# A graph layer on one core: loads three ahead and evictions two behind in a background job, and zero rows written one at a time beside another job

## The chip, the cores and the metric

The kernel runs on one core of a Trainium2 chip. The metric is the device time of one execution in microseconds; the median of the runs is given. Times that are read off a profile come from one profiled execution. The engines are PE (matrix multiply; PEld is its weight load), DVE (vector), ACT (scalar functions), POOL (here the issuer of the indirect DMAs) and SP (the issuer of the plain DMAs).

## The reference

For 6250 nodes with 256 features, and 206,250 edges sorted by destination, the layer computes:

```
xn = layernorm(x)
q, k, v = xn Wq + bq, xn Wk + bk, xn Wv + bv            (8 heads of 32)
per edge (src -> dst): sim = q[dst] . k[src] * scale;  p = softmax over the edges of dst
agg[dst] = sum of p * v[src];  gnn = agg Wo + bo
mix: linear attention over all nodes, 8 heads of 64: k and v instance-normalised,
     dots = k^T v, out = q dots / N, then its projection
x  = x + gnn + mix
h  = layernorm(x); each node goes to the one of 8 experts with the largest logit
     (capacity 977); y = (relu(h W1 + b1) W2 + b2) * probability
out = x + y
```

## The kernel before

**Blocks and groups.** The nodes stand in 49 blocks of 128, in three groups of 20, 17 and 12 blocks. First a node stage (to about 137 us) computes keys and values of all blocks into the DRAM table `kv_tab`, the queries of the first group alone, and sorts the first group's nodes by degree. Then the attention over edges runs through the blocks of group 0, 1 and 2. In a group's blocks the nodes stand in order of degree, so that a block needs a planned number of edge slots `S`.

**Units and chunks.** A block with more than 44 slots is cut into units; a unit is cut into chunks of at most 5 slots (`W`), seven or eight chunks a unit. Per slot POOL issues one indirect gather of 128 rows (2 KB: key and value) into one of 11 (`RING`) buffers `kvg` (line 627). DVE multiplies the chunk's keys with the query (L1373) and reduces over the heads (L1374); this is the score. When all chunks of a unit are scored comes its softmax (L1379 to L1404, with ACT's exponential L1391). In the next unit's chunks DVE weighs the values chunk by chunk (`weigh`, L1325) and PE adds them up with an identity matrix (L1329), which frees the ring's buffer. `complete` then makes `ag` (L1347) and `send` scatters it to `agg_tab` (L843, on POOL's queue). POOL's program holds the gathers up to two chunks (`LEAD`) beyond the one that is scored ahead of that scatter.

**Background jobs.** All other work is written as generators in a list `jobs`, which are taken in order, one after the other. Before and after the weighing of each chunk the main loop calls `background(work / 2)`. Each `yield n` of a job costs n credits; `background` runs jobs while it has credit, and sets the credit to zero when the list is empty. `pace` (L1295) gives the credit per slot: for group 0 it is 1.1 x 363.8 (`work_beside(0)`) over 693 slots, so 0.58 a slot and 2.9 a chunk of five. Nothing but this order and the semaphores decides when an instruction runs[...].

For group 0 the jobs are:

1. `other_queries` (L649): the queries of blocks 20 to 48. Per block: SP loads the transposed block `xTm` (L661, 128 KB, two buffers), PE multiplies it in two halves (L672) into a PSUM bank (five buffers, shared by all jobs), DVE scales and adds the bias into `qn` (L675, two buffers), and SP stores it to `q_tab` (L678). A turn for block b loads b + 1, multiplies b and evicts b - 1.
2. `other_ranks` (L681): orders groups 1 and 2 by degree, mostly DVE work (L282 to L362, `over` L687).
3. `zero_rows` (L692): writes zeros to the DRAM buffers `xbuf` that the experts' tokens are scattered into later. Three rows of 1 KB per partition and write, so 30 writes of 384 KB or less on SP (L701), one credit each, 11.1 MB in all.
4. `linear_attention` (L704): loads its weights `wm`, subtracts column means (L727 to L729) and row means (L233), then for 49 blocks loads `xTm` (L719), projects (L751), squares on ACT, takes variances on DVE (L768 to L777), scales on ACT and multiplies (L788). A step is two yields of 2.4.

When a group's last block is sent, the job `behind(g)` is appended: output projection, routing, scatter to `xbuf` (`to_tiles`), the experts, and `finish`. It runs beside the attention of the next group; that of the last group runs alone after the attention.

Of the kernel before, what the change touches and what calls it, by code (L numbers as in the profile page):

```python
# [9 lines left out]
F32 = mybir.dt.float32  # L10
# [3 lines left out]
ALU = mybir.AluOpType  # L14
# [4 lines left out]
P = 128  # L19
# [9 lines left out]
GROUPS = (20, 17, 12)  # L29
# [39 lines left out]
def gps_layer(  # L69
# [34 lines left out]
    nc = tc.nc  # L104
    N, D = x.shape
    E = n_edges
    NB = -(-N // P)
# [6 lines left out]
    DC = D // P  # L114
# [3 lines left out]
    NX, _, F = w1.shape  # L118
# [14 lines left out]
    def q_rows(b):  # L133

        i = b - FIRST_OF[group_of[b]]
        return q_tabs[group_of[b]][i * P : (i + 1) * P, :]

    def bcast_row(ap, n, parts=P):
        return bass.AP(tensor=ap.tensor, offset=ap.offset, ap=[[0, parts], [1, n]])
# [18 lines left out]
    with tc.manual_schedule():  # L158
# [36 lines left out]
        rstd = keep.tile([P, NB], F32, name="rstd")  # L195
# [8 lines left out]
        def x_transposed(to, b, n=1, queue=nc.sync):  # L204

            queue.dma_start(to, xT_all[:, b * DC * P : (b + n) * DC * P])
# [7 lines left out]
        def bank(shape):  # L214

            t = bps.tile([P, 512], F32, name="bank")
            n = math.prod(shape)
            v = t[:, :n]
            if len(shape) == 2:
                v = v.rearrange("p (a b) -> p a b", a=shape[0])  # L220
            if len(shape) == 3:
                v = v.rearrange("p (a b c) -> p a b c", a=shape[0], b=shape[1])
            return v

        def less_mean(w, n):

            for c0 in range(0, n, 512):
                m = min(512, n - c0)
                pw = bank((m,))
                for c in range(DC):  # L230
                    nc.tensor.matmul(pw, ones_d, w[:, c, c0 : c0 + m], start=(c == 0), stop=(c == DC - 1))
                for c in range(DC):
                    nc.vector.tensor_sub(w[:, c, c0 : c0 + m], w[:, c, c0 : c0 + m], pw)  # L233


        jobs = []
# [408 lines left out]
        bctx = ExitStack()  # L645
        mp1 = bctx.enter_context(tc.tile_pool(name="m1", bufs=1))
        mp2 = bctx.enter_context(tc.tile_pool(name="m2", bufs=2))

        def other_queries():  # L649

            wq = mp1.tile([P, DC, D], F32, name="wqn")
            for c in range(DC):
                nc.sync.dma_start(wq[:, c, :], w_node[c * P : (c + 1) * P, 2 * D : 3 * D])
            bq = mp1.tile([P, D], F32, name="bqn")
            nc.sync.dma_start(bq, bcast_row(b_node[2 * D :], D))
            xT_of, pq_of = {}, {}

            def load(b):
                if b < NB:
                    xT_of[b] = mp2.tile([P, DC, P], F32, name="xTm")  # L660
                    x_transposed(xT_of[b].rearrange("p c q -> p (c q)"), b)  # L661

            load(GROUPS[0])
            yield 2.0
            less_mean(wq, D)
            yield 2.0
            for b in range(GROUPS[0], NB + 1):
                load(b + 1)
                if b < NB:
                    pq_of[b] = bank((D,))  # L670
                    for c in range(DC):
                        nc.tensor.matmul(pq_of[b], xT_of[b][:, c, :], wq[:, c, :], start=(c == 0), stop=(c == DC - 1))  # L672
                if b > GROUPS[0]:
                    q = mp2.tile([P, D], F32, name="qn")
                    nc.vector.scalar_tensor_tensor(  # L675
                        q, pq_of.pop(b - 1), rstd[:, b - 1 : b], bq, op0=ALU.mult, op1=ALU.add
                    )
                    nc.sync.dma_start(q_rows(b - 1), q)  # L678
                yield 1.0

        def other_ranks():  # L681
            t = rank_consts(mp1)
            for g in range(1, NG):
                yield from rank_group(g, t, mp1, mp2)
            bs = list(range(NB))
            for b in bs:
                nc.vector.tensor_scalar(over[:, b : b + 1], deg_r[:, b : b + 1], float(SLOTS[b]), None, op0=ALU.is_gt)  # L687
                if b % 8 == 7:
                    yield 1.5
            nc.vector.tensor_reduce(bad[:, 1:2], over, AX.X, ALU.max)  # L690

        def zero_rows():  # L692

            zero = mp1.tile([P, D], F32, name="zero")
            nc.vector.memset(zero, 0.0)
            for g in range(NG):
                n_r = TILES[g] * SIZE[g] // P
                view = xbufs[g][0 : n_r * P, :].rearrange("(p r) d -> p r d", p=P)
                for r in range(0, n_r, 3):
                    n = min(3, n_r - r)  # L700
                    nc.sync.dma_start(view[:, r : r + n, :], zero[:, None, :].to_broadcast([P, n, D]))  # L701
                    yield 1.0

        def linear_attention():  # L704
# [9 lines left out]
            xT_of = {}  # L714

            def load(b):
                if b < NB:
                    xT_of[b] = mp2.tile([P, DC, P], F32, name="xTm")
                    x_transposed(xT_of[b].rearrange("p c q -> p (c q)"), b)  # L719
# [26 lines left out]
            def project(b):  # L746
                pms[b] = []
                for s in range(2):
                    pm = bank((MI,))
                    for c in range(DC):  # L750
                        nc.tensor.matmul(  # L751
                            pm, xT_of[b][:, c, :], wmf[:, c, s * MI : (s + 1) * MI],
                            start=(c == 0), stop=(c == DC - 1),
                        )
                    pms[b].append(pm)

            def squares(b):
                sqs[b] = mp2.tile([P, G, MD], F32, name="sq")
                for s in range(2):
                    nc.scalar.activation(  # L760
                        sqs[b][:, s * MH : (s + 1) * MH, :].rearrange("p g d -> p (g d)"), pms[b][s], AF.Square
                    )
                cvs[b] = mp2.tile([P, MI], F32, name="cv")
                nc.scalar.copy(cvs[b], pms[b][1])

            def variances(b):
                rv = mp2.tile([P, G], F32, name="rv")
                nc.vector.tensor_reduce(rv, sqs[b], AX.X, ALU.add)  # L768
                nc.vector.tensor_scalar(rv, rv, rs2[:, 1, b : b + 1], EPS, op0=ALU.mult, op1=ALU.add)
                rks[b] = mp2.tile([P, MH], F32, name="rk")  # L770
                nc.vector.tensor_mul(rks[b], rv[:, :MH], rv[:, MH:])
                nc.scalar.activation(rks[b], rks[b], AF.Sqrt)

            def scaled(b):
                rk = rks[b]
                nc.vector.reciprocal(rk, rk)
                nc.vector.tensor_scalar(rk, rk, rs2[:, 0, b : b + 1], None, op0=ALU.mult)  # L777
                cks[b] = mp2.tile([P, MH, MD], F32, name="ck")
                for h in range(MH):
                    nc.scalar.activation(  # L780
                        cks[b][:, h, :], pms[b][0][:, h * MD : (h + 1) * MD], AF.Copy, scale=rk[:, h : h + 1]
                    )

            def products(b):
                ckf = cks[b].rearrange("p h d -> p (h d)")
                for hp in range(HP):
                    h = slice(hp * P, (hp + 1) * P)
                    nc.tensor.matmul(  # L788
                        dots[:, hp, :], cvs[b][:, h], ckf[:, h],
                        start=(b == 0 and hp == 0), stop=(b == NB - 1 and hp == HP - 1),  # L790
                        skip_group_check=True,
                    )

            for i in range(NB + 2):
                if 2 <= i:
                    products(i - 2)
                load(i + 1)
                if i < NB:
                    project(i)
                if 1 <= i <= NB:  # L800
                    variances(i - 1)
                yield 2.4
                if i < NB:
                    squares(i)
                if 1 <= i <= NB:
                    scaled(i - 1)
                yield 2.4

            wq = mp1.tile([P, HP, D], F32, name="wq")
            nc.sync.dma_start(wq, w_mixq.rearrange("(h p) d -> p h d", p=P))  # L810
            wot = mp1.tile([P, HP, D], F32, name="wot")
# [470 lines left out]


        jobs.append(other_queries())
        jobs.append(other_ranks())
        jobs.append(zero_rows())
        jobs.append(linear_attention())

        def work_beside(g):
# [672 lines left out]
```

## Time and profile before

| what | value |
|---|---|
| median of 3 runs | 3531.13 us (3529.72 to 3541.31) |
| profiled execution, its own time | 3071.36 us |
| span, first to last instruction | 3069.6 us |
| PE busy | 2217.7 us (72%) |
| DVE busy | 2026.7 us (66%) |
| POOL busy | 1923.8 us (63%), 2114 instructions |
| ACT busy | 638.1 us (21%) |
| DMA | 728.05 MB, mean 237 GB/s |
| mean granted PE clock | 0.855 |

The profiled execution is 460 us shorter than the median of the runs. The busy times are averages over stages. In the trace the first key and value gather starts at 138.4 us, the queries job runs to 241 us, the ranks to 351 us, the zero rows are issued from 352 to 397 us, and the linear attention follows. A line of the timeline gives start, length, engine, line, operation and count, and in brackets how long the engine was idle before, and what released it.

### The profile page before, as it was taken

How to read it: one execution, taken by the hardware profiler on the slowest of the kernel's cores; microseconds unless marked ns; L12 is line 12 of the kernel's file. 1: busy time of each engine (PE TensorE's matmuls, PEld its weight loads, DVE VectorE, ACT ScalarE, POOL GpSimd, SP SyncE). 2: the span in 40 equal slices, each digit the busy share in tenths (PEclk: the TensorE clock that was granted, in tenths of full speed). 3: DMA queues.
4: the chain of work that ended last, by engine and by line, in shares of the span. 5: the costliest groups of instructions: out<-in, count | busy, mean ns of one | idle time of the engine just before them, and what ended most of it. 6: DMA issues, size and time to landing. Idle time of an engine off the chain costs nothing. (4 is left out here: it accounts for less than half of the span.)

```text
span 3069.6 us, 29584 instructions
## 1 busy us (share of the span) xinstructions
PE 2217.7 (72%) x9090; PEld 1731.0 (56%) x9090; DVE 2026.7 (66%) x2728; ACT 638.1 (21%) x1800; POOL 1923.8 (63%) x2114
## 2 busy tenths in 40 slices
PE   8756548788788655764989988445629999856494
PEld 4335335555555444643777877334528888735494
DVE  5658868898888767884767766566845666664000
ACT  4300003343434101210111111101202122112242
POOL 4366767777777777567777777776466767650101
PEclk9867779999898778876999999678859999978797
DMA  7675876777777668767888887777668988753783
GB/s 256 212 248 171 268 260 201 213 211 213 208 206 221 199 197 262 250 195 234 307 285 307 294 301 248 223 204 248 198 188 279 321 300 311 241 179 111 279 327 111
DMA packets 294378, 728.05 MB, mean 237 GB/s; under 512 B 47142, under 2 KB 156292, under 8 KB 280900
## 3 DMA queue, kind: packets, MB, share of 16 engines
q0 software_dynamic: 149744, 477.83, 50.7%
q1 hardware_dynamic: 144468, 248.24, 23.2%
q8 instruction: 75, 1.23, 0.2%
q14 instruction: 91, 0.75, 0.1%
HBM read 652.25 MB, written 73.64 MB: 236 GB/s over the span
## 5 line engine op out<-in xcount | busy, mean ns | idle before, releaser
L627 POOL DMA_INDIRECT kvg<-kv_tab,idx x1715 | 1628.3, 949 | 650.7 <-issue 463.2
L1329 PE MATMUL pa<-kvg,ident 128*128 128x256 f32 x3430 | 1008.4, 451 | 583.3 <-DVE kvg L1325 420.6
L1329 PEld LDWEIGHTS pa<-kvg,ident 128*128 128x128 f32 x3430 | 756.9, 227 | 817.1 <-DVE kvg L1325 501.4
L1373 DVE TENSOR_TENSOR kvg<-kvg,qc 128x1280 f32<-128x1280 f32 (+1 forms) x366 | 512.4, 1400 | 389.3 <-DMA kvg<-kv_tab,idx 326.7
L1374 DVE TENSOR_REDUCE sim<-kvg 128x40 f32<-128x1280 f32 (+1 forms) x366 | 513.2, 1402 | 12.6
L1325 DVE TENSOR_TENSOR kvg<-kvg,pr 128x1280 f32<-128x1280 f32 (+1 forms) x366 | 509.3, 1393 | 0.0
L1204 PE MATMUL bank<-wt,hTe 128*128 128x256 f32 x1056 | 247.7, 382 | 0.0
L1187 PE MATMUL bank<-xTe,wt 128*128 128x256 f32 x1056 | 242.6, 381 | 2.3 <-ACT xTe L1177 2.3
L1187 PEld LDWEIGHTS bank<-xTe,wt 128*128 128x128 f32 x1056 | 201.6, 191 | 30.5 <-ACT xTe L1177 3.0
L1204 PEld LDWEIGHTS bank<-wt,hTe 128*128 128x128 f32 x1056 | 201.7, 193 | 27.5
L1268 DVE TENSOR_TENSOR res<-bank,row_b 128x256 f32<-128x256 f32 x49 | 20.6, 421 | 280.8 <-ACT bank L1264 272.6
L751 PE MATMUL bank<-wm,xTm 128*128 128x512 f32 x392 | 178.0, 597 | 0.0
L1247 POOL DMA_INDIRECT row_a<-ybuf,row_from x49 | 46.5, 948 | 197.6 <-DMA ybuf<-res 173.0
L1193 ACT ACTIVATE hTe<-bank,wt 128x256 f32<-128x256 f32 x264 | 110.8, 471 | 266.0 <-PE bank L1187 266.0
L1210 ACT COPY res<-bank 128x256 f32<-128x256 f32 x85 | 31.7, 372 | 424.5 <-PE bank L1208 236.1
L751 PEld LDWEIGHTS bank<-wm,xTm 128*128 128x128 f32 x392 | 72.1, 194 | 71.6 <-issue 71.3
L1301 ACT COPY qc<-qs 128x256 f32<-128x256 f32 x49 | 18.8, 384 | 442.9 <-DVE kvg L1373 412.0
L843 POOL DMA_INDIRECT xbuf<-row_a,row_to x49 | 48.0, 980 | 96.6 <-DVE cmp L1088 67.5
L537 PE MATMUL pkv<-wn,xT 128*128 128x512 f32 (+1 forms) x276 | 106.0, 540 | 3.5 <-DVE kv L552 3.5
L843 POOL DMA_INDIRECT agg_tab<-ag,node_ri x49 | 48.5, 990 | 91.2 <-DVE ag L1347 68.4
L1173 PE MATMUL bank<-ident,in 128*128 128x128 f32 x170 | 28.7, 283 | 100.4 <-DMA in<-xbuf 100.4
L780 ACT ACTIVATE ck<-bank,rk 128x64 f32<-128x64 f32 x392 | 86.2, 341 | 28.9 <-DVE rk L777 28.4
(258 smaller groups left out, 2208.4 us busy)
## 6 DMA issues: line engine op xcount, KB each, us to landing
wt<-in_w_rows_dram SPq DMA_DIRECT2D x33, 1152.0 KB, 8.2
wt<-in_w_rows_dram SPq DMA_DIRECT2D x33, 1028.0 KB, 7.9
kvg<-kv_tab,idx POOLq DMA_INDIRECT x1715, 4.0
kvg<-in_w_rows_dram SPq DMA_DIRECT2D x19, 1152.0 KB, 6.1
kvg<-in_w_rows_dram SPq DMA_DIRECT2D x19, 1028.0 KB, 7.7
kv_tab<-kv SPq DMA_DIRECT2D x49, 256.0 KB, 2.7
in<-xbuf SPq DMA_DIRECT2D x85, 128.0 KB, 8.7
ybuf<-res SPq DMA_DIRECT2D x85, 128.0 KB, 3.4
```

Of the source, the lines that this page charges most:

```text
L537: nc.tensor.matmul(done[i], xTs[b // GX][:, b % GX, c, :], wn[:, c, w], start=(c == 0), stop=(c == DC - 1))
L627: nc.gpsimd.indirect_dma_start(out=kv[:, j - j0, :], out_offset=None, in_=kv_tab[:, :], in_offset=bass.IndirectOffsetOnAxis(ap=idx_of[b][: ...
L751: nc.tensor.matmul(pm, xT_of[b][:, c, :], wmf[:, c, s * MI : (s + 1) * MI], start=(c == 0), stop=(c == DC - 1),)
L780: nc.scalar.activation(cks[b][:, h, :], pms[b][0][:, h * MD : (h + 1) * MD], AF.Copy, scale=rk[:, h : h + 1])
L843: s = nc.gpsimd.indirect_dma_start(**kw)
L1187: nc.tensor.matmul(ph[:, k, :], w[:, c, f * P : (f + 1) * P], T[t]["xT"][:, c, :size], start=(k == 0 and c == 0), stop=(k == 1 and c == DC ...
L1193: nc.scalar.activation(T[t]["hT"][:, f, :size], ph[:, k, :], AF.Relu, bias=w1_t[:, V1 + f : V1 + f + 1])
L1204: nc.tensor.matmul(py, T[t]["hT"][:, f, k * P : (k + 1) * P], w[:, f, :], start=(f == 0), stop=False)
L1325: nc.vector.tensor_tensor(vals, vals, v["pr"][:, j0 - s0 : j1 - s0, :, None].to_broadcast([P, m, GH, GD]), ALU.mult)
L1329: nc.tensor.matmul(v["pa"], ident, kv[:, j, D:], start=(j0 + j == s0), stop=(j0 + j == s1 - 1),)
L1373: nc.vector.tensor_tensor(keys, keys, qc[:, None, :].to_broadcast([P, j1 - j0, D]), ALU.mult)
L1374: nc.vector.tensor_reduce(sim[:, j0 - s0 : j1 - s0, :], keys.rearrange("p j (h d) -> p j h d", d=GD), AX.X, ALU.add)
```

## The change

In `other_queries` the loads get a pool of four buffers of their own (`xTq`) and run three blocks ahead of the matmul instead of one; the eviction and the store are two blocks behind it instead of one, with one more turn of the loop and so one more credit. `zero_rows` is no longer a job of its own: `linear_attention` takes one of its 30 writes at the start of each of its 51 steps, ahead of that step's load of `xTm`, and what is left at the end. The writes themselves are the same, and cost no credits now. `work_beside(0)`, and with it the pace, is unchanged.

```diff
         mp2 = bctx.enter_context(tc.tile_pool(name="m2", bufs=2))
+        mp4 = bctx.enter_context(tc.tile_pool(name="m4", bufs=4))
...
             def load(b):
                 if b < NB:
-                    xT_of[b] = mp2.tile([P, DC, P], F32, name="xTm")
+                    xT_of[b] = mp4.tile([P, DC, P], F32, name="xTq")
                     x_transposed(xT_of[b].rearrange("p c q -> p (c q)"), b)
 
-            load(GROUPS[0])
+            for b in range(GROUPS[0], GROUPS[0] + 3):
+                load(b)
             yield 2.0
             less_mean(wq, D)
             yield 2.0
-            for b in range(GROUPS[0], NB + 1):
-                load(b + 1)
+            for b in range(GROUPS[0], NB + 2):
+                load(b + 3)
                 if b < NB:
                     pq_of[b] = bank((D,))
                     for c in range(DC):
                         nc.tensor.matmul(pq_of[b], xT_of[b][:, c, :], wq[:, c, :], start=(c == 0), stop=(c == DC - 1))
-                if b > GROUPS[0]:
+                if b > GROUPS[0] + 1:
                     q = mp2.tile([P, D], F32, name="qn")
                     nc.vector.scalar_tensor_tensor(
-                        q, pq_of.pop(b - 1), rstd[:, b - 1 : b], bq, op0=ALU.mult, op1=ALU.add
-                    )
-                    nc.sync.dma_start(q_rows(b - 1), q)
+                        q, pq_of.pop(b - 2), rstd[:, b - 2 : b - 1], bq, op0=ALU.mult, op1=ALU.add
+                    )
+                    nc.sync.dma_start(q_rows(b - 2), q)
                 yield 1.0
...
+            zeros = zero_rows()
             for i in range(NB + 2):
+                next(zeros, None)
                 if 2 <= i:
                     products(i - 2)
                 load(i + 1)
...
+            for _ in zeros:
+                pass
             wq = mp1.tile([P, HP, D], F32, name="wq")
...
         jobs.append(other_queries())
         jobs.append(other_ranks())
-        jobs.append(zero_rows())
         jobs.append(linear_attention())
```

## The prediction

> **What bounds the kernel now.** I first read the groups of instructions, to see which engine has the longest row.
>
> ```profile
> L627 POOL DMA_INDIRECT kvg<-kv_tab,idx x1715 | 1628.3, 949 | 650.7 <-issue 463.2
> ```
>
> POOL issues 1715 gathers of key and value rows, 949 ns each, with about 0.30 us of "issue" behind each: one gather per 1.25 us. Next come the windows over group 0, where the changed jobs lie (columns: stretch, its length, busy us and instructions of PE, PEld, DVE, ACT and POOL, PE clock, DMA share, GB/s).
>
> ```profile
> 240.00:265.00 25.00, 14.45 (x54) 11.20 (x54) 22.56 (x43) 0.38 (x1) 11.02 (x11) 0.80 0.47 142
> 375.00:400.00 25.00, 12.54 (x35) 8.64 (x33) 15.87 (x12) 0.00 (x0) 15.93 (x17) 0.74 1.06 392
> 500.00:600.00 100.00, 83.43 (x311) 55.53 (x310) 92.54 (x114) 40.66 (x121) 76.02 (x82) 0.95 0.72 212
> ```
>
> From 500 to 600 us POOL starts 82 instructions in 100 us, that is one per 1.22 us: its full pace, so POOL bounds this stage (DVE, at 92.5 us, is close behind). At 240 to 265 us it starts 11 in 25 us and at 375 to 400 us 17; the full pace gives 20. POOL's timeline between 138 and 500 us names each gap (start, length, instruction, in brackets the idle time before it and its releaser).
>
> ```profile
> 213.60 0.94 POOL L627 DMA_INDIRECT kvg<-kv_tab,idx  x1 [10.50 <-PE pa L1329]
> ...
> 228.14 0.94 POOL L627 DMA_INDIRECT kvg<-kv_tab,idx  x1 [3.33 <-PE pa L1329]
> ...
> 237.57 0.95 POOL L627 DMA_INDIRECT kvg<-kv_tab,idx  x1 [4.73 <-PE pa L1329]
> ...
> 265.12 1.00 POOL L843 DMA_INDIRECT agg_tab<-ag,node_ri  x1 [10.98 <-DVE ag L1347]
> ...
> 373.96 0.97 POOL L627 DMA_INDIRECT kvg<-kv_tab,idx  x1 [3.50 <-DVE kvg L1325]
> ...
> 394.19 0.94 POOL L627 DMA_INDIRECT kvg<-kv_tab,idx  x1 [4.27 <-DMA kvg<-kv_tab,idx]
> ...
> 416.76 0.94 POOL L627 DMA_INDIRECT kvg<-kv_tab,idx  x1 [5.37 <-PE pa L1329]
> ...
> 466.94 0.94 POOL L627 DMA_INDIRECT kvg<-kv_tab,idx  x1 [3.17 <-PE pa L1329]
> ```
>
> Less the usual 0.30 us each, and with four small ones (0.56, 0.44, 2.47 and 0.52, 0.81 us, the first three by PE pa), the stalls are: while the queries job runs 10.2 + 0.3 + 3.0 + 4.4 = 17.9 us on the ring and 10.7 at the scatter, 28.6 in all; in the ranks job 2.3; in the zero rows 3.2 + 4.0 + 5.1 = 12.3; at the start of the linear attention 3.6. Sum 46.8 us. From 474 to 1240 us there is no further gap above 0.32 us, so what POOL wins early is kept to the end of group 0.
>
> Why is POOL late at 213 us? It waits for a slot of the eleven-slot ring, which PE's L1329 frees after DVE's work. The waits from 138 to 265 us (us in total, times, longest) and DVE's timeline show why DVE is late.
>
> ```profile
> DVE qn L675 <- PE bank L672: 31.4, 16, 4.8
> PE bank L672 <- DMA xTm<-in_xT_all_dram: 30.5, 12, 5.2
> ```
> ```profile
> 201.59 0.48 DVE L675 SCALAR_TENSOR_TENSOR qn<-bank,rstd,bqn 128x256 f32<-128x256 f32 x1 [4.77 <-PE bank L672]
> 201.99 1.48 DVE L1373 TENSOR_TENSOR kvg<-kvg,qc 128x1280 f32<-128x1280 f32 x1
> ```
>
> DVE stands at the eviction L675 for its matmul, and the matmul for a load issued just before; the eighth chunk's score L1373 is queued behind it at 201.99 us, although its last gather ended at 184.3 us and lands some 4 us later, at 188. Last, the DMA view of 350 to 400 us, and of 500 to 700 us (size, median us to landing).
>
> ```profile
> xbuf<-zero SPq DMA_DIRECT2D x27, 384.0 KB, 9.0
> kvg<-kv_tab,idx POOLq DMA_INDIRECT x32, 7.3
> ```
> ```profile
> kvg<-kv_tab,idx POOLq DMA_INDIRECT x148, 3.8
> ```
>
> The zero rows are sent in one burst (392 GB/s) and a gather then takes 7.3 us instead of 3.8; DVE starves, falls behind, and POOL stalls.
>
> **What the Trainium skill says.** "DMA: Bandwidth & Descriptors", section "Issuing engines are not separate DMA queues": transfers of all issuers share the same 16 engines and interleave. The trace agrees: SP's zeros delay POOL's gathers by 3.5 us. Its "Rules for kernel authors" say to issue a DMA early and wait late; the xTm loads, 3.8 us to landing, are issued too late here, and 30.5 us of PE waits agree. "Perfetto Trace Analysis", section "Per-engine timelines", calls ACT, DVE and GpSimd strict FIFO: L1373 behind L675 at 201.99 us agrees.
>
> **The queries job.** Work is the same: 29 loads, 116 matmuls, 29 evictions, 29 stores; one more turn of the loop. With four buffers and three loads ahead, PE always finds a landed block: at 0.58 credits a slot a turn comes every 1.25 / 0.58 = 2.2 us, so a load has some 6.5 us for its 3.8. Evictions stand two behind, so the L672 waits go. What is late next: the store buffer qn still has two slots. In the first unit evictions come in threes, and the third must wait for the first one's store (4.1 us to landing, q_tab from qn): about 3.4 us in each of three such threes. Followed by hand, chunk by chunk (landing of the gathers, 3.0 us of scoring, 0.47 us an eviction), the eighth score starts at about 193 us with these waits, at 189 without them, instead of 202: 9 to 13 us earlier. From there to the scatter's input `ag` DVE took 202.0 to 264.8 us; 9.6 us of that were L672 waits (1.63 + 0.61 + 3.50 + 1.98 + 1.84), which go, and about one 1.5 us step of the ranks is placed later, one eviction of 0.5 more comes in. So `ag` comes at 264.8 - 9 - 9.6 - 1.0 = 245 us, or 241. POOL without stalls would be there at 138.4 + 78 x 1.25 = 236 us, so it still waits. Saving: 20 to 24 us; I take **22**.
>
> **The ranks.** From 265 to 351 us DVE is busy nearly without a gap, so this stretch is only shifted, with the postponed step in it: **+1.5**.
>
> **The zero rows.** The burst goes and its 12.3 us of stalls with it: **-12.3**. The linear attention starts 30 credits (some 10 chunks) earlier, hence straight behind the ranks: DVE has had no pause and meets 5.3 us of column means L727 to L729, 2.6 us of L233 and a 4.2 us wait for PE with less slack; before, that cost 3.6 us: **+1.5**, from 0 to 6.
>
> **The zero writes beside the linear attention.** 30 writes, each 384 KB or less, one per step of 4.8 credits, or 10.4 us. 11.1 MB over 312 us adds 36 GB/s to 212; the share rises from 0.72 to about 0.83, so there is room. On SP's queue the zero write stands ahead of the load of the next xTm, which is needed a step (10 us) later; hidden, and 1.5 us a write if it were not. But a write takes the engines about 384 KB / 392 GB/s = 1.0 us, in which a gather is late. If DVE is not waiting for that gather this is nothing; if it is, DVE loses up to 1 us of its 8 us of slack per 100. No run of before shows a lone write: the bound is 0 from below (a write helps no one), and from above the 3.5 us that the burst put on a gather, 30 x 3.5 = 105. I take 0.13 us each, **+4**: most fall where DVE has slack.
>
> Sum: -22 + 1.5 - 12.3 + 1.5 + 4 = **-27 us**. The instructions of groups 1 and 2 keep their order on every engine, so that the saving goes to the end. The profiled execution took 3071.4 us (span 3069.6 and 1.8 around it): 3044 is expected of it. The median of the runs is 3531, 460 us longer than the profiled one, and the trace doesn't say where these 460 are; I carry the saving over as it is (scaled by 3531 / 3071 it would be 31): **3504 us**.
>
> **Rivals.**
> - *Nearly all stalls go.* The threes of evictions don't wait, or saving scales: -24 - 12 + 1 = -35, by 1.15 -40: 3491 to 3496. For it: gathers that land sooner let DVE start sooner. Against: DVE is busy 22.6 of 25 us at 240 to 265 us.
> - *DVE takes the place of the wait.* DVE's work is the same and close to POOL's pace (92.5 to 100), so what is won at 265 us is lost again in ranks and means, for want of the pause that the zeros gave. Half remains: 3517.
> - *No change.* Later groups wait for other things, or the longer unprofiled runs have their bound elsewhere: 3524 to 3537.
> - *Slower.* The lone zero writes delay gathers through all of the linear attention, where POOL had no stall. Without their cost the change gives -31, so from 31 / 30 = 1.0 us per write it loses, from (31 + 10.6) / 30 = 1.4 us by over 0.3%. At 2 us: 3531 - 31 + 60 = 3560. For it: 3.5 us in the burst. Against: DMA share 0.72 there.
>
> **How the numbers follow.** Forecast 0.50 (3494 to 3514), all stalls 0.15, half remains 0.17 (mostly above 3514), no change 0.11, slower 0.07. The range leaves out most of the slower case and the far end of the fast one: 3484 to 3526. 0.3%, or 10.6 us, is about what a measurement of this kernel can tell from no change. Faster: 0.50 + 0.15 + most of 0.17 = 0.79; same 0.14; slower 0.07.
>
> **What would show it.** Right: no L675-like wait on PE's query matmuls, or under 5 us; the first scatter to agg_tab at 241 to 246 us; no gap of POOL from 350 to 420 us above 2 us; gathers landing in about 4 us there. Wrong: POOL's gaps between 340 and 700 us adding up to over 20 us (the zero writes or the means), the scatter still after 255 us, or the end of group 0 earlier but the end of the program not.

## The result and the profile after

The changed kernel took 3505.21 us in the median of 20 runs (3485.04 to 3519.66), the kernel before 3532.05 (20 runs, 3513.34 to 3542.71): ratio 0.9926, 95% interval 0.991 to 0.9943, or 26 us less by the ratio. The forecast was 3504.

In some sets of runs the kernel before takes 3505 to 3532 us and in others 3067 to 3069 us, so every run is compared with the kernel before of its own set alone. I call the first kind A (the result, and e1 to e4) and the second kind B (e5 to e12). The profile of before that the prediction worked with, 3069.6 us long, is of kind B; the profile after, 3504.3 us long (own time 3506.13), is of kind A. These two can't be laid side by side. First, the group of gathers and a window of the changed kernel in kind A (columns of the window as in the prediction):

```profile
L627 POOL DMA_INDIRECT kvg<-kv_tab,idx x1715 | 1624.9, 947 | 895.7 <-issue 497.4 <-PE pa L1334 179.9 <-remote 112.2
```
```profile
500.00:600.00 100.00, 74.49 (x252) 49.91 (x252) 74.24 (x88) 29.74 (x92) 64.99 (x70) 0.85 0.70 210
```

A gather takes POOL 947 ns as before (949), but the idle time ahead of the gathers is 895.7 us, not 650.7. From 500 to 600 us POOL starts 70 instructions, not 82: in kind A it is not at its full pace in this stage, where the prediction had it at full pace.

To check the prediction step by step, the changed kernel was profiled in kind B (e9 below, span 3054.8). Its windows, and the gaps of POOL's timeline that answer to those of before:

```profile
375.00:400.00 25.00, 17.27 (x56) 10.38 (x55) 17.36 (x22) 4.83 (x10) 16.75 (x18) 0.98 0.76 238
500.00:600.00 100.00, 82.72 (x312) 55.81 (x311) 90.40 (x112) 40.12 (x119) 75.86 (x83) 0.95 0.80 246
```
```profile
140.96 0.94 POOL L627 DMA_INDIRECT kvg<-kv_tab,idx  x1 [27.47 <-issue]
...
224.91 0.94 POOL L627 DMA_INDIRECT kvg<-kv_tab,idx  x1 [2.27 <-PE pa L1334]
...
254.00 1.00 POOL L849 DMA_INDIRECT agg_tab<-ag,node_ri  x1 [9.75 <-DVE ag L1352]
...
328.13 0.94 POOL L627 DMA_INDIRECT kvg<-kv_tab,idx  x1 [5.29 <-PE pa L1334]
...
367.25 0.97 POOL L627 DMA_INDIRECT kvg<-kv_tab,idx  x1 [4.26 <-PE pa L1334]
...
376.81 0.94 POOL L627 DMA_INDIRECT kvg<-kv_tab,idx  x1 [4.84 <-PE pa L1334]
...
403.81 0.94 POOL L627 DMA_INDIRECT kvg<-kv_tab,idx  x1 [3.54 <-PE pa L1334]
```

The long gap at 213 us (10.5) is gone; small ones of about 2 us stand in its place. The zeros' gaps at 374, 394 and 417 us are gone too, but there are three others at 367, 377 and 404 us, just as long. At 500 us POOL has its full pace (83 instructions). Now the DMA view of 350 to 400 us:

```profile
xbuf<-zero SPq DMA_DIRECT2D x4, 384.0 KB
kvg<-kv_tab,idx POOLq DMA_INDIRECT x31, 3.7
```

Four zero writes instead of 27 lie there, and a gather lands after 3.7 us instead of 7.3, as predicted. So the burst's cost to the gathers went, and POOL still stalls.

For all runs of kind B the same four times can be read off POOL's timeline (us; a stall is a gap less the usual 0.30; the fourth column counts from 85 to 240 us behind the first scatter, where zero rows, column means and the start of the linear attention lie; the fifth is the time from the first gather to the 400th):

| kernel | first gather to first scatter | stalls in the next 85 us | stalls after that | 400th gather | ratio of times |
|---|---|---|---|---|---|
| before (first profile) | 126.7 | 2.3 | 15.8 | 582.1 | 1 |
| e9 changed | 113.0 | 5.2 | 14.3 | 570.5 | 0.9954 |
| e10 queries only | 113.2 | 4.8 | 17.4 | 572.4 | 0.997 |
| e11 zeros only | 123.8 | 2.1 | 20.5 | 584.2 | 1.0016 |
| e5 changed, 8 store buffers | 105.4 | 4.3 | 17.8 | 564.5 | 0.9935 |
| e6 before, 8 store buffers | 123.7 | 2.0 | 19.0 | 582.3 | 1.0001 |
| e7 changed, zeros twice | 115.2 | 4.5 | 16.6 | 573.9 | 0.9966 |
| e8 changed, pause in front of the loop | 114.5 | 4.5 | 9.8 | 566.0 | 0.9942 |
| e12 changed, 8 buffers and pause | 105.2 | 4.4 | 8.4 | 553.8 | 0.9915 |

The 400th gather tells almost the whole saving: -11.6 us for the changed kernel, -28.3 for e12, against -14 and -26 in the times (1 less the ratio, times 3067). In the second and fourth column differences of some 3 us can't be read: with one and the same queries job the first scatter comes after 126.7 us in before and 123.8 in e11, and the three kernels that keep the burst have 15.8, 17.4 and 19.0 us of stalls in the fourth column.

### The profile page after: what moved, and what is told of

Read it like the earlier page. It is cut to its first block, busy times and chain, and to the rows that moved or that the text cites. A ratio compares the mean times of both kernels' runs of the same rounds, so it can differ in the third digit from the quotient of the medians.

```text
span 3504.3 us, 29584 instructions
## 1 busy us (share of the span) xinstructions
PE 2321.5 (66%) x9090; PEld 1776.2 (51%) x9090; DVE 2025.7 (58%) x2728; ACT 628.5 (18%) x1798; POOL 1920.6 (55%) x2114
## 4 chain that ended last, share of the span: by engine, by line
PE 38%; issue 19%; DVE 15%; POOL 11%; another core or an unknown queue 8%; DMA 5%; ACT 2%; SPq 0%; DVEq 0%; POOLq 0%; ACTq 0%
PE pa L1334 12%; POOL kvg L627 9%; PE bank L1193 8%; PE bank L1210 8%; DVE kvg L1378 4%; DVE sim L1379 3%; DVE kvg L1330 3%; PE pkv L537 2%; DMA kvg<-kv_tab,idx 2%; PE bank L753 2%; PE bank L914 1%; PE bank L1214 1%; PE bank L790 1%; DVE rv L770 1%
## 5 line engine op out<-in xcount | busy, mean ns | idle before, releaser
L627 POOL DMA_INDIRECT kvg<-kv_tab,idx x1715 | 1624.9, 947 | 895.7 <-issue 497.4
L1334 PE MATMUL pa<-kvg,ident 128*128 128x256 f32 x3430 | 1028.1, 455 | 639.0 <-issue 417.8
L1334 PEld LDWEIGHTS pa<-kvg,ident 128*128 128x128 f32 x3430 | 768.5, 230 | 877.3 <-issue 496.8
L1379 DVE TENSOR_REDUCE sim<-kvg 128x40 f32<-128x1280 f32 (+1 forms) x366 | 513.3, 1402 | 12.6
L1193 PE MATMUL bank<-xTe,wt 128*128 128x256 f32 x1056 | 267.9, 402 | 38.8 <-issue 36.3
L1210 PE MATMUL bank<-wt,hTe 128*128 128x256 f32 x1056 | 265.5, 396 | 40.7 <-issue 39.2
L1352 DVE TENSOR_TENSOR ag<-pa,s 128x256 f32<-128x256 f32 x46 | 19.5, 424 | 349.9 <-PE pa L1334 212.6
L753 PE MATMUL bank<-wm,xTm 128*128 128x512 f32 x392 | 199.9, 657 | 1.3 <-issue 1.2
L790 PE MATMUL bank<-ck,cv 128*128 128x128 f32 x392 | 74.0, 342 | 107.4 <-ACT ck L782 95.8
L790 PEld LDWEIGHTS bank<-ck,cv 128*128 128x128 f32 x392 | 67.8, 243 | 121.0 <-ACT ck L782 102.1
L770 DVE TENSOR_REDUCE rv<-sq 128x16 f32<-128x1024 f32 x49 | 59.5, 1215 | 120.0 <-ACT sq L762 103.9
L762 ACT ACTIVATE sq<-bank 128x512 f32<-128x512 f32 x98 | 56.3, 595 | 363.3 <-remote 180.3
```

The costliest lines, as they stand in the source:

```text
L627: nc.gpsimd.indirect_dma_start(out=kv[:, j - j0, :], out_offset=None, in_=kv_tab[:, :], in_offset=bass.IndirectOffsetOnAxis(ap=idx_of[b][: ...
L753: nc.tensor.matmul(pm, xT_of[b][:, c, :], wmf[:, c, s * MI : (s + 1) * MI], start=(c == 0), stop=(c == DC - 1),)
L790: nc.tensor.matmul(dots[:, hp, :], cvs[b][:, h], ckf[:, h], start=(b == 0 and hp == 0), stop=(b == NB - 1 and hp == HP - 1), skip_group_ch ...
L1193: nc.tensor.matmul(ph[:, k, :], w[:, c, f * P : (f + 1) * P], T[t]["xT"][:, c, :size], start=(k == 0 and c == 0), stop=(k == 1 and c == DC ...
L1210: nc.tensor.matmul(py, T[t]["hT"][:, f, k * P : (k + 1) * P], w[:, f, :], start=(f == 0), stop=False)
L1334: nc.tensor.matmul(v["pa"], ident, kv[:, j, D:], start=(j0 + j == s0), stop=(j0 + j == s1 - 1),)
```

## The experiments

### The kernel before once more, and the two halves (e1 to e4, kind A)

e1 is the kernel before, unchanged.

> The kernel before, unchanged, for a second profile: its first profile spans 3069.6 us while its runs take 3532. If the two profiles differ because of how the execution went and not because of the kernel, this one spans some 3505 to 3540 us, and its POOL has gaps of 2 to 4 us in the linear attention that the first profile does not have. If the first profile stands for all executions, it spans 3070 us again.

Measured: 3506.28 us against 3505.22, ratio 0.9999 (0.998 to 1.0017). Its profile spans 3514.1 us, so the length of the first profile, 3069.6, is not the kernel's alone; POOL's waits at the scatters are up to 14.9 us long here.

e2 keeps the new queries job and gives the zero rows their own job back:

```
-            zeros = zero_rows()
...
-                next(zeros, None)
...
-            for _ in zeros:
-                pass
...
+        jobs.append(zero_rows())
```

> Half of the change: loads three ahead and evictions two behind, and the zero rows stay a job of their own ahead of the linear attention. My theory (two savings that add up, queries 22 us, zero rows 12.3 less 5.5 to 7 given back): -18 to -24 us against the kernel before. Rival 1 (DVE takes the place of the wait, so queries alone give nothing lasting): 0 to -8. Rival 2 (all of the gain is the zero rows'): 0.

Measured: ratio 0.9975 (0.9959 to 0.999), 9 us less, with an interval of 4 to 14: half of the 18 to 24 expected.

e3 is the kernel before with the zero writes taken into the linear attention (the same lines the other way round).

> The other half: the zero rows one at a time beside the linear attention, the queries job as before. My theory: 12.3 us of stalls go, 1.5 come back at the column means and 4 at the lone writes: -4 to -12 us. Rival 1 (the pause of 30 credits was of use to DVE, and its loss costs what the burst cost): -3 to +5. Rival 2 (all of the gain is here): -24 to -30.

Measured: ratio 0.9971 (0.9957 to 0.9985), 10 us less.

e4 is the changed kernel.

> The changed kernel, unchanged, for a second profile and for its time beside the two halves on the same chip: about 27 us shorter than the kernel before in time. Its profile is about 27 us shorter than that of e1 if both are of the same kind; if one of them comes out near 3050, the difference between the two kinds of profile is not the kernel's.

Measured: 3476.33 us, ratio 0.9931 (0.9906 to 0.9956), 24 us less. The halves make 19 us together, which the interval of e4 (15 to 33) holds. So in kind A both halves gain, the queries some 9 of their 22. The profile, 3471.6 us long, is 42 us shorter than that of e1, but the first profile of the same changed kernel (3504.3) only 10.

What holds the queries job is seen in the timeline of e4 from 199 to 220 us (SPq: a transfer that SP issues):

```profile
199.56 0.33 SPq L206 DMA_DIRECT2D xTq<-in_xT_all_dram  x1
199.56 0.48 DVE L677 SCALAR_TENSOR_TENSOR qn<-bank,rstd,bqn 128x256 f32<-128x256 f32 x1 [10.71 <-remote]
...
203.62 2.04 PE L674 MATMUL bank<-wqn,xTq 128*128 128x256 f32 x4 [8.98 <-issue]
...
210.76 0.33 SPq L206 DMA_DIRECT2D xTq<-in_xT_all_dram  x1
210.76 0.48 DVE L677 SCALAR_TENSOR_TENSOR qn<-bank,rstd,bqn 128x256 f32<-128x256 f32 x1 [7.80 <-remote]
...
219.17 0.48 DVE L677 SCALAR_TENSOR_TENSOR qn<-bank,rstd,bqn 128x256 f32<-128x256 f32 x1 [7.92 <-remote]
```

From 179 to 219 us the job does one block in 8 to 11 us, although in the program its loads are three blocks ahead; e1 has the same pitch there (180.63, 191.12, 201.63, 212.82). "remote" says only that the view names no releaser. The expectations of the next two runs put this crawl down to the store of two blocks before, since the store buffer has two slots. The trace of e4 speaks against that. A load of `xTq` starts at the same moment as the eviction, and what the load waits for is the matmul that frees its buffer, no store. The trace also holds the moments at which semaphores move, the counters by which one engine tells another that it is done: DVE's wait for the store before the eviction at 210.76 is over at 203.80, and PE's semaphore moves at 210.74. Counted in program order this eviction is that of the ninth block, whose matmuls are recorded as ended at 176.86. So in kind A the job waits for PE's report, here 34 us after the recorded end.

This holds for all profiles. In the nine of kind B PE's semaphore moves within 40 ns of the recorded end of a matmul, in all but the last 3 of 2617 to 2619 moves. In the five of kind A 548 to 625 of the 2052 to 2094 moves that the traces hold come over 1 us after the last such end, up to 24 us; for DVE and ACT that is so in 1 to 3 moves. The ends of matmuls are modelled in a profile, so that it can't be told whether the matmul ends late or only its report, and why is not shown.

### The store buffers (e5, e6, kind B)

e5 is the changed kernel, e6 the kernel before, each with

```
+        mpq = bctx.enter_context(tc.tile_pool(name="mq", bufs=8))
...
-                    q = mp2.tile([P, D], F32, name="qn")
+                    q = mpq.tile([P, D], F32, name="qs")
```

> The changed kernel with eight store buffers for the queries instead of two; nothing else. Theory A (from about 180 to 220 us an eviction of the queries job waits until the store two evictions before it has reported, so that the job does one block in 10 to 11 us, although its loads are early): with eight buffers this crawl is gone, the evictions of these 40 us come 1 to 3 us apart, the first scatter to agg_tab comes 8 to 25 us earlier than at 289 us, and the end 8 to 20 us earlier than that of the changed kernel, ratio to the kernel before 0.988 to 0.991. Theory B (the loads, or TensorE at half clock, hold the job): evictions still 10 to 11 us apart, end within 4 us of the changed kernel, ratio 0.992 to 0.994.

> The kernel before with eight store buffers for the queries, loads still one block ahead. Theory A: the store, not the load, holds the job, so the buffers alone bring at least what the longer prefetch brought (9 us), 10 to 20 us, ratio 0.994 to 0.997. Theory C (both hold it in turn: with the store out of the way the load issued just before is what is waited for): 3 to 8 us. Theory B: nothing, ratio 0.999 to 1.001.

Measured: e5 3049.02 us against 3068.61, ratio 0.9935 (0.9921 to 0.9949), 20 us less; e6 ratio 1.0001 (0.9989 to 1.0013). What DVE waited for from 138 to 265 us (us in total, times, longest), with one line of PE's, in before, e9, e5 and e6:

```profile
DVE qn L675 <- DMA q_tab<-qn: 3.4, 2, 2.8
```
```profile
DVE qn L677 <- DMA q_tab<-qn: 22.6, 15, 2.8
PE bank L674 <- DMA xTq<-in_xT_all_dram: 10.6, 7, 4.8
...
DVE kvg L1378 <- DMA kvg<-kv_tab,idx: 4.7, 2, 3.3
```
```profile
DVE kvg L1379 <- DMA kvg<-kv_tab,idx: 20.3, 11, 3.5
...
DVE qs L678 <- PE bank L675: 0.3, 1, 0.3
```
```profile
DVE qs L676 <- PE bank L673: 32.3, 18, 3.4
```

Before, DVE stood 31.4 us at the evictions for PE and 3.4 for a store. The change took the wait for PE away and put 22.6 us of waits for the store in its place, 15 times. With eight buffers (e5) nothing is left of it: DVE now waits for gathers, 11 times, and POOL has no stall on the ring from its first gather on; it waits 8.0 us at the first scatter itself. That comes 105.4 us after the first gather, 21.3 earlier than before. With eight buffers but late loads (e6) the old wait for PE stays whole, and the time is unchanged. At the scatter early loads bring 13.7 us, both edits 21.3, buffers alone 3.0, which is no more than e11 has without any change to this job.

The times by themselves don't decide between the theories. Theory B had "nothing" for e6, and that is what came; e5's 0.9935 lies in B's range too, but both ranges assumed 0.993 for the changed kernel. Against its 0.9954 in kind B (e9, another set) e5 gains 6 us, with an uncertainty of some 6. The waits decide for kind B: the load is the first wait in the row and the store the second, so neither theory holds as it was written. Neither run was made in kind A, where by e4's trace the evictions of the crawl wait for PE.

The Trainium skill, "DMA: Bandwidth & Descriptors", section "Anatomy of one DMA", gives a DMA that GpSimd issues 2.0 us of fixed cost, mostly the receipt of the write, and the bytes by 436 GB/s; the section has no such sum for SP's. Taken over to SP's store of 128 KB it would be an estimate of 2.3 us. The profile of before has 4.1 us, beside the gathers. The measured one decides: with two slots, evictions that come in threes wait for it.

### The zero writes twice (e7, kind B)

```
                     nc.sync.dma_start(view[:, r : r + n, :], zero[:, None, :].to_broadcast([P, n, D]))
+                    nc.sync.dma_start(view[:, r : r + n, :], zero[:, None, :].to_broadcast([P, n, D]))
```

> The changed kernel with each of the 30 zero writes beside the linear attention sent twice, one behind the other on SyncE's queue (the rows are zeroed twice, nothing else). If a lone write is hidden, as the prediction has it (0.13 us each), the end moves by 0 to 4 us against the changed kernel. If a lone write delays the gathers that VectorE waits for, it costs about 1 us each, 25 to 35 us, ratio about 1.000.

Measured: ratio 0.9966 (0.9953 to 0.9979), against 0.9954 of the changed kernel (e9, another set): 4 us more, with an uncertainty of some 6. The 400th gather is 3.4 us later. 25 to 35 us are excluded: a second write behind each costs about 0.1 us, 0.3 at most. That the first one costs no more is inferred from it, since leaving the writes out altogether was not tried (the rows are read later). The rival that had the change slower by 2 us a write falls.

### The pause (e8, kind B)

```
             zeros = zero_rows()
+            for _ in range(30):
+                yield 1.0
             for i in range(NB + 2):
```

> The changed kernel with the 30 turns of the old zero-rows job kept as empty turns ahead of the linear attention (VectorE has its pause again, the writes still go out one at a time in the linear attention). If the linear attention meets VectorE with too little slack since it starts earlier (the +1.5 us of the prediction, at most 6), this is 1 to 6 us faster than the changed kernel. If the pause was worth nothing it is the same within 3 us. If the earlier start of the linear attention is itself a gain, since its work spreads over more chunks, it is 3 to 10 us slower.

Measured: ratio 0.9942 (0.9928 to 0.9955), 18 us less than before, some 4 less than the changed kernel; the times of the two sets overlap, but the profile is plain: POOL's stalls after the ranks are 9.8 us, where no kernel without burst and pause has under 14.3. As it was built, this pause lies behind the column means and ahead of the loop over the blocks; its 9.8 us are those of the means alone (gaps at 367, 376 and 384 us), and those of the loop's start are gone.

### The changed kernel, its halves and a better one (e9 to e12, kind B)

e9, e10 and e11 are e4, e2 and e3 once more.

> The changed kernel beside the kernel before once more, to have it on the same chip as the next three. On the chip of the last runs (some 3069 us before): the first scatter comes 115 us after the first gather, as in the runs with two store buffers, not 127 as before (-12); the zero rows' burst no longer stalls POOL (-12), but the column means meet VectorE without slack (+6) and so does the start of the linear attention's loop (+5): -10 to -17 us, ratio 0.9945 to 0.9967. If the prediction's sum were right, -27, ratio 0.991. On the chip of the first runs (some 3510 us before): as measured there, 0.993.

> The queries job of the change alone, the zero rows still in their own job ahead of the linear attention. On the chip of the last runs: the first scatter 115 us after the first gather, and this kept to the end, -11 to -13 us, ratio 0.996; by the prediction -22, ratio 0.993. On the chip of the first runs: -9 us as there.

> The zero writes beside the linear attention alone, the queries job as before. By the prediction -12.3 + 1.5 + 4 = -7 us, ratio 0.998. By the theory that the pause was worth more than the burst's stalls cost (column means +6, start of the loop +5): -3 to +1 us, ratio 0.999 to 1.0005. On the chip of the first runs: -10 us as there.

Measured: e9 3053.65 us against 3067.12, ratio 0.9954 (0.9939 to 0.9969), 14 us less; e10 0.997 (0.9959 to 0.998), 9 us less; e11 1.0016 (1.0006 to 1.0026), 5 us more, beyond what either theory had. The two halves make -4 together, the whole -14: they are not independent here. Why is not shown. The table says this much: in the stalls after the ranks, the kernels with the burst (15.8, 17.4, 19.0) and those with neither burst nor pause (14.3, 16.6, 17.8, 20.5) lie in one range, so that giving up both saves POOL nothing there that can be told.

What stalls POOL in the place of the burst is seen in the timeline of DVE and PE of e9 (start, length, in brackets the idle time ahead):

```profile
359.33 1.21 DVE L729 TENSOR_REDUCE wmean<-wm 128x16 f32<-128x1024 f32 x1
360.57 0.17 DVE L730 TENSOR_SCALAR wmean<-wmean 128x16 f32<-128x16 f32 x1
360.78 1.22 DVE L731 TENSOR_TENSOR wm<-wm,wmean 128x1024 f32<-128x1024 f32 x1
...
361.92 1.22 DVE L1330 TENSOR_TENSOR kvg<-kvg,pr 128x1024 f32<-128x1024 f32 x1
...
363.19 3.78 PE L1334 MATMUL pa<-kvg,ident 128*128 128x256 f32 x8 [17.41 <-DVE kvg L1330]
...
369.77 1.28 DVE L233 TENSOR_TENSOR wm<-wm,bank 128x512 f32<-128x512 f32 x2 [3.60 <-PE bank L231]
370.98 1.48 DVE L1330 TENSOR_TENSOR kvg<-kvg,pr 128x1280 f32<-128x1280 f32 x1
...
372.51 4.02 PE L1334 MATMUL pa<-kvg,ident 128*128 128x256 f32 x10 [2.77 <-DVE kvg L1330]
```

From 265 to 350 us DVE was busy for 78.1 of 85 us, and the means (349.5 to 362.0 us) follow the ranks, which end at 343.6, without a pause. POOL's gap of 4.26 us that ends at 367 us is not yet a matter of L233: the weighing that frees its slot, at 361.92, stands behind a softmax and the second half of the means, and then comes PE's adding, to 366.97. The gap of 4.84 us at 377 us belongs to the weighing at 370.98, which stands behind DVE's wait of 3.60 us at L233, and the adding after it. This adding takes 3.78 us for 8 matmuls and 4.02 for 10, where it takes 1.99 and 2.43 at 389.7 and 381.0 us: from 350 to 380 us the granted clock is 0.63, from 380 to 410 us 0.94. So a slow PE has a part in both gaps, which the runs don't separate. In the kernel before the means ran at 435 us and later, behind the pause, with only one wait at L233 (4.2 us), and there too the granted clock was low (0.61 from 410 to 440 us, 0.80 from 440 to 470). In e11 the waits at L233 are largest, and POOL's gaps too; the second and third of these follow them:

```profile
DVE wm L233 <- PE bank L231: 11.0, 2, 5.9
```
```profile
375.00 0.97 POOL L627 DMA_INDIRECT kvg<-kv_tab,idx  x1 [4.93 <-PE pa L1332]
...
386.18 0.94 POOL L627 DMA_INDIRECT kvg<-kv_tab,idx  x1 [6.46 <-PE pa L1332]
...
398.22 0.94 POOL L627 DMA_INDIRECT kvg<-kv_tab,idx  x1 [6.10 <-PE pa L1332]
```

e12 takes what e5 and e8 point to: the eight store buffers of e5, and the pause, now ahead of the means:

```
             load(0)
             yield 2.4
             yield 2.4
+            for _ in range(30):
+                yield 1.0
```

> The changed kernel with eight store buffers for the queries, and with 30 empty turns ahead of the linear attention's column means (the old job's pause without its writes). On the chip of the last runs: first scatter 105 us after the first gather (-21), and POOL's gaps from 350 to 500 us add up to under 6 us instead of 16 (-10): -28 to -33 us, ratio 0.989 to 0.991, faster than the changed kernel and than it with eight buffers alone (0.9935). If the pause brings nothing: as that one, 0.993 to 0.994. On the chip of the first runs: at most the changed kernel's 0.993, if its stores and its pause are not what holds it there.

Measured: 3041.89 us, ratio 0.9915 (0.9896 to 0.9933), 26 us less: about twice the gain of the changed kernel (0.9954) in the same set. This is a little short of the 28 to 33 us expected, and POOL's gaps are not under 6 us. Its timeline from 320 to 480 us has one gap above 2 us:

```profile
439.60 0.94 POOL L627 DMA_INDIRECT kvg<-kv_tab,idx  x1 [5.82 <-PE pa L1337]
```

It follows the means (407 to 434 us; one wait of 6.3 us for L231), so that even with the pause they cost some 6 us, not the 3.6 of before. Against eight buffers without the pause (e5, another set) the time is 6 us less, with an uncertainty of some 7, and the 400th gather comes 10.7 us earlier. e12 was not run in kind A.

## Why the prediction was right in its sum and wrong in its terms

The median fell within 2 us of the forecast. The sum was made for the profile of kind B, and there it is half of what was said: -14 us (9 to 19) for -27. That the runs of kind A gave -26 is no proof of the terms: as far as the runs show, it is luck.

- *Queries, "-22": the wait was read rightly, its successor was too small.* The waits for PE's query matmul are gone in e9. But the first scatter came 113.0 us after the first gather, not 105: 13.7 us earlier than before, where 22 were forecast. The term that is too small is "about 3.4 us in each of three such threes": there are 15 waits for a store, 22.6 us in all. With them taken away (e5) the gain at the scatter is 21.3 us, so the rest of the step comes out in its sum. (All these gains are some 3 us smaller if e11, with the old queries job, is taken as their base.) "PE always finds a landed block" did not hold: PE still waits for loads, 7 times, 10.6 us in all, but DVE's wait for PE is gone all the same.
- *Ranks, "+1.5".* The stalls there rose from 2.3 to 5.2 us: +2.9.
- *Zero rows, "-12.3".* The burst is gone, and its landing times of 7.3 us too: right.
- *Column means, "+1.5, from 0 to 6": wrong, and outside its bounds.* Without the pause, means and loop start stall POOL by 14.3 us (14.3 to 20.5 in e9, e7, e5 and e11) where they stalled it by 3.6: +10.7, nearly all of the 12.3 that went with the burst. The prediction saw that "DVE has had no pause" and priced it from a place where DVE had one. By the profiles it is the pause: with it, the stalls of the two are 8.4 us in e12, with the same buffers but no pause (e5) 17.8. The pause also puts the means some 70 us later in the attention; how much of the gain is the pause and how much the place was not separated.
- *Lone zero writes, "+4".* e7: 4 us (with 6 either way) for 30 more of them. Not contradicted, as far as can be told.
- *No gap above 2 us from 350 to 420 us, scatter at 241 to 246 us:* both failed in e9; gathers landing after 4 us held. In kind B the rival "DVE takes the place of the wait", with -14 us, is what came out. Its reason holds for the means and, less, for the ranks; the 8 us that are missing at the scatter are the store's, which it didn't name.
- *"I carry the saving over as it is":* the step was not sound. In kind A the zero half alone gains 10 us (e3), in kind B it loses 5 (e11), and the intervals exclude each other. What POOL waited for from 480 to 1560 us in kind A, e1 and then e3:

```profile
POOL agg_tab L843 <- DVE ag L1347: 102.5, 14, 14.9
```
```profile
POOL agg_tab L847 <- DVE ag L1350: 80.3, 11, 21.1
```

In kind B POOL has hardly a stall from 500 to 1200 us (0 to 0.6 us in all runs); in kind A POOL waits at the scatters all through the linear attention, 22 us less in e3 than in e1. But e2 has 105.9 us, and the two profiles of the changed kernel have 86.2 (e4) and 96.3, and are 20 us apart at the 850th gather, about as much as is to be explained. So the profiles hint that the gain of kind A lies in part in a stage in which the prediction expected none; this is not shown, and where the 26 us come from in kind A stays open.

## What to carry to other kernels

When a load is moved ahead, follow the buffer behind it as well: the evictions come closer together, and a store buffer of two slots then takes the place of the load. A job that only issues DMAs is also a pause for the engine that the jobs around it keep busy, here DVE; price its removal at what the next job costs without slack, not at what it cost with it. And before a saving is carried from a profile to the runs, see that the profiled execution is as long as they are.

## What the runs showed that was not expected

The same kernel takes 3069.6 us in one profiled execution and 3514.1 in another (e1), with the same instructions: a gather takes POOL 949 and 951 ns, a score's reduction on DVE 1402 ns in both. The idle time ahead of the gathers is 650.7 and 880.5 us. PE's clock is 0.855 and 0.814, and a matmul of the experts (L1187) takes 381 and 404 ns. The difference lies in the waits, above all. By the semaphores, as told for e4, PE's reports come late in kind A alone; in e1, 27 idle times of DVE and 20 of POOL end just after such a late report, 169 and 63 us in all. What makes them late, no run here tells. The record names the chip of three sets: e1 to e4 ran on one (kind A), e5 to e8 and e9 to e12 on two others (kind B). The kind may go with the chip; no chip was tried twice.

An edit can have opposite signs in the two: 0.9971 and 1.0016 for the zero writes.
